# Destinations of sorted expert rows from one load and a one-hot product, one register for three tiles, nine result buffers, the shared expert last

## The chip, the cores and the metric

The kernel runs on 1 core of one Trainium2 chip. The metric is device microseconds of one execution. Three runs of the kernel before gave 907.51, 905.93 and 907.47 us, median 907.47. A profile covers one further execution; its times count from the start of its span. Engines: TensorE (PE, its weight loads PEld), VectorE (DVE), ScalarE (ACT), GpSimd (POOL) and SyncE (SP). SP computes nothing here: it issues most of the DMAs. "SPq" is its queue.

## The reference

One transformer block, B = 8 batches of 256 channels by 512 values; for the second half each channel is one token of width 512.

```python
x = x + cross_attention(layernorm(x), ctx, mask)            # 16 heads of 16, softmax over 512 source positions
flat = layernorm(x).reshape(-1, 512)                        # 2048 tokens
shared = sigmoid(flat @ shared_gate.T) * (flat @ shared_up.T) @ shared_down.T      # float32, hidden 352
weights = softmax(flat @ router_w.T)                        # 8 experts
top_w, top_idx = top_k(weights, 2)
routed = sum over e of comb[:, e] * (sigmoid(xb @ wg[e].T) * (xb @ wu[e].T)) @ wd[e].T   # bfloat16
return x + layernorm(x) + shared + routed                   # as the kernel's accumulator holds it: acc = x + norm(x)
...
```

Every token goes through the shared expert; of the eight routed experts it needs only its two.

## The kernel before

**Attention.** Steps are numbered by (G, h): G = 0 to 31 is a quarter of a batch's heads, h = 0 to 7 a step in it. A step does one `row_max` (L416: a score product of two matmuls into one PSUM bank, then DVE's maximum, L424) for a coming group, one `exp_scores` (L438) for this group, and on some steps `attend`, the projections or the parts of the feed-forward work of the batch before. `row_max` R = 8 (G+1) + h + LEAD runs LEAD = 2 steps ahead. A `plan` of 32 lists a batch hands out the further work: `spread` (L949) puts the items of `shared_units` (one item is one matmul group of the shared expert, 30 per batch) and of `route` (the routing of a batch) on chosen steps. For the last batch the steps of the shared expert's first 24 items stand in SOONER (L944); the other six follow behind the attention (L1112 to L1117).

**Sorting.** For the first 15 half batches of tokens (NS = 15, 128 tokens each) `route` works out, on DVE, each token's two experts and its two rows in a list sorted by expert. `place` (L643) then scatters with indirect DMAs from POOL: the token's 512 bfloat16 values to `xs`, and two words, its place in the result and its weight, to the same row of `whose`. The 16th half batch isn't sorted. `expert_map` (L666) works out for each of NT = 37 tiles of 128 sorted rows its expert (packed eight to a register) and its first row (`M["row"]`, L715).

**Tiles.** `expert_tiles` (L719) goes over the 37 tiles. `fetch(t)` (L727) runs on SP's queue: it loads first rows into registers in pieces (L733: 2, 8, 12 and 15 of them), then issues a transposing DMA of the tile (L739, `late_ctx<-xs`, four buffers, three tiles ahead), and a small DMA of the tile's 128 places and weights (L741, `whom<-whose`, six buffers). `gate_up_of` (L757) does the two products `eg` and `eu` and DVE's gated product `hz` (L771), `turn_h` (L778) turns `hz` on PE (L781), `down_of` (L788) multiplies by the down weights (`ey`, L795), ACT scales by the weight (L802) and POOL scatters the rows to `zs` (L803, traced as L201). PE's order is gate and up of t, down of t-2, turn of t-1.

**The end.** `give_back` (L818): POOL loads 12 accumulators back (`again`, L833, 256 KB each); `results(n)` (L835) loads the two result rows of 128 tokens from `zs` (three buffers, on SP, L837); `add` (L839) adds them on DVE (L842) and the write of the output follows on SP (L844). The order at the end is: 37 tiles; the shared expert of the last batch (L864, L915; 12 products of 4 matmuls, then two halves of 3); then the 16th half batch, dense, through all eight experts (`dense`, weights applied on ACT, L775, and DVE, L776), summed in one PSUM bank. The additions start in the middle of the shared expert and are placed by estimated time: at most 28 of the 30 during the shared expert, one for each 0.78 us of estimated PE work. `again` is issued at one per round of three items from round six on.

PSUM banks for the tiles come from a ring of six (`bank`, L80). One call of `bank` moves it on by one.

Of the kernel before, what the change touches and what calls it, by code (L numbers as in the profile page):

```python
# [36 lines left out]
def xattn_ffn_kernel(  # L37
# [137 lines left out]
    for i in range(8):  # L175
        nc.gpsimd.memset(eights[:, i : i + 1], float(8**i))
    tv = const.tile([P, NT], F32, name="tv")
    nc.gpsimd.iota(tv, [[1, NT]], channel_multiplier=0, allow_small_or_imprecise_dtypes=True)
# [11 lines left out]

    xs = dram.tile([E * ROWS + P, T], BF16, name="xs")
    whose = dram.tile([E * ROWS + P, 2], I32, name="whose")
    gu16 = dram.tile([E, 2, I, T], BF16, name="gu16")
# [356 lines left out]
    def route(b, tts=(0, 1)):  # L550
# [61 lines left out]
        def share():  # L612

            w16 = one.tile([P, n, E], BF16, tag=f"r{n}_comb16", name="comb16")
            nc.vector.tensor_copy(w16, t["w"])
            part = one.tile([P, 2, n, E], F32, tag=f"r{n}_part", name="part")
            nc.vector.scalar_tensor_tensor(part, both, 0.5, of_choice(w16), ALU.mult, ALU.mult)
            t["who"] = who = two.tile([P, 2, n, 2], I32, tag=f"r{n}_who", name="who")
            nc.vector.reduce_sum(who[:, :, :, 1].bitcast(F32), part, axis=AX.X)
            nc.vector.tensor_scalar(  # L620
                who[:, :, :, 0], place0[:, :, tts[0] : tts[0] + n], float(b * C), None, ALU.add
            )
            t["h16"] = h16 = one.tile([P, n, E], BF16, tag=f"r{n}_h16", name="h16")
            nc.vector.tensor_add(h16, t[0], t[1])
# [36 lines left out]

    PACKED = (NT + 7) // 8
    NEXT = [base0]
    M = {}

    def expert_map():  # L666
# [39 lines left out]
        def rows():  # L706
            step = sm("step", [E - 1])
            nc.vector.tensor_sub(step, t["shift"][:, 1:], t["shift"][:, : E - 1])
            past = t["past"]
            nc.vector.tensor_mul(past, past, row8(step).to_broadcast([P, NT, E - 1]))  # L710
            r = sm("r", [NT])
            nc.vector.reduce_sum(r, past, axis=AX.X)
            nc.vector.scalar_tensor_tensor(r, tv, float(P), r, ALU.mult, ALU.subtract)
            M["row"] = ri = one.tile([P, NT], I32, tag="m_ri", name="ri")
            nc.vector.tensor_scalar(ri, r, float(E * ROWS), None, ALU.min)  # L715

        return [(0.0, f) for f in (tiles, ends, experts, rows)]

    def expert_tiles():  # L719

        XT, HT, WHO = {}, {}, {}
        AHEAD = 3
        PIECES = [(0, 2), (2, 10), (10, 22), (22, NT)]
        ROW, EIGHT = {}, {}
        whole = {}

        def fetch(t):  # L727

            if t >= NT:
                return  # L730
            for first, end in PIECES:
                if t == first:
                    _, rs = nc.values_load_multi_w_load_instructions(  # L733
                        M["row"][0:1, first:end], engines=(mybir.EngineType.SP,), min_val=0, max_val=E * ROWS
                    )
                    ROW.update(zip(range(first, end), rs))
            row = ROW.pop(t)
            XT[t] = late("ctx")[:, t % 4, :].rearrange("p (k n) -> p k n", n=P)
            nc.sync.dma_start_transpose(out=XT[t], in_=xs[bass.ds(row, P), :])  # L739
            WHO[t] = six.tile([P, 2], I32, tag="who", name="whom")  # L740
            nc.sync.dma_start(out=WHO[t], in_=whose[bass.ds(row, P), :])  # L741

# [14 lines left out]
        def gate_up_of(t):  # L757
            whole.pop(t, None)
            xT = XT.pop(t) if t < NT else S[B - 1]["xTb"]
            pg = bank([P, I], F32, "eg")  # L760
            pu = bank([P, I], F32, "eu")
            for m, ps in ((0, pg), (1, pu)):
                for kc in range(NKC):
                    nc.tensor.matmul(  # L764
                        ps, xT[:, kc, :], weights_of(t, guT, m, kc, slice(None)),
                        start=(kc == 0), stop=(kc == NKC - 1),
                    )
            th = two.tile([P, I], F32, tag="th", name="eth")
            nc.scalar.activation(th, pg, AF.Tanh, scale=0.5)  # L769
            if t < NT:  # L770
                nc.vector.scalar_tensor_tensor(HZ[t % 2], th, 1.0, pu, ALU.add, ALU.mult)  # L771
                fetch(t + AHEAD)
            else:
                w = S[B - 1]["comb"][:, 0, t - NT : t - NT + 1]
                nc.scalar.activation(th, th, AF.Identity, scale=w, bias=w)  # L775
                nc.vector.tensor_mul(HZ[t % 2], th, pu)  # L776

        def turn_h(t):  # L778
            ps = bank([P, 3, P], BF16, "pht")
            for ic, (i0, n) in enumerate(ECH):  # L780
                nc.tensor.transpose(ps[:, ic, :], HZ[t % 2][:, i0 : i0 + n], identb)  # L781
            HT[t] = two.tile([P, 3, P], BF16, tag="hT", name="hT")
            if t < NT:
                evacuate(HT[t], ps)
            else:
                nc.scalar.copy(HT[t], ps)

        def down_of(t):  # L788
# [10 lines left out]
            if t < NT:  # L799
                y = (late("mb", 2)[:, t % 5, :] if t % 5 < 2 else late("xm")[:, t % 5 - 1, :])  # L800
                who = WHO.pop(t)
                nc.scalar.activation(y, ps, AF.Copy, scale=who[:, 1:2].bitcast(F32))  # L802
                scatter(zs, who[:, 0:1], y, bounds_check=2 * ROWS - 1, oob_is_err=False)  # L803

# [10 lines left out]

        return lambda: [fetch(t) for t in range(AHEAD)], stream(0, NT), stream(NT, NT + E)

    def give_back():  # L818
# [9 lines left out]
        byrow = zs.rearrange("(c r) t -> r c t", c=2)  # L828
        Z = {}

        def again(b, tt):
# [3 lines left out]
        def results(n):  # L835
            Z[n] = three.tile([P, 2, T], BF16, tag="extra", name="z")
            nc.sync.dma_start(out=Z[n], in_=byrow[n * P : (n + 1) * P])  # L837

        def add(n, c):  # L839
            b, tt = halves[n]  # L840
            a = S[b]["acc", tt]
            nc.vector.tensor_add(a, a, Z[n][:, c, :])  # L842
            if c == 1:
                nc.sync.dma_start(out=out[b, tt * P : (tt + 1) * P, :], in_=a)  # L844

# [6 lines left out]
    def shared_units(b, own):  # L852
# [58 lines left out]
        def down(tt, ic):  # L911
# [6 lines left out]
            if ic == 2:  # L918
                acc = s["acc", tt]
                nc.vector.scalar_tensor_tensor(acc, t["y"], 0.5, acc, ALU.mult, ALU.add)  # L920
                if b < NB - 1:
                    nc.sync.dma_start(out=ACC[b][tt], in_=acc)

        return (
# [20 lines left out]
        (8, 2), (9, 2), (10, 1), (11, 3),  # L945
        (13, 2), (15, 3), (17, 2), (19, 3), (21, 3), (23, 2), (25, 1),
    ]
# [63 lines left out]
    nc.gpsimd.memset(blank, 0.0)  # L1011
    nobody = five.tile([P, E * NS + 1, 2], I32, tag="acc", name="nobody")
    nc.gpsimd.memset(nobody, NOWHERE)

# [13 lines left out]
    for b in range(B):  # L1028
# [15 lines left out]
        elif b == B - 1:  # L1044
# [4 lines left out]
            sorted_last = route(b, (0,)) + expert_map()  # L1049
            fetch, tiles, dense = expert_tiles()  # L1050
            spread(plan, sorted_last, [(23, 1), (24, 1), (25, 2), (26, 3), (27, 2), (28, 2), (29, 2), (30, 1)])
            plan[30].append(fetch)
        later = plan[STEPS:]
        plan = plan[:STEPS]
        for g in range(NG):
            G = NG * b + g
            for h in range(8):
                st, half = divmod(h, 2)
                R = 8 * (G + 1) + h + LEAD
                if R // 8 < last:  # L1060
                    row_max(R // 8, (R % 8) // 2, R % 2)
                exp_scores(G, st, 1 - half, "s2" if R // 8 < last else ("s1", "s2")[h % 2])
# [52 lines left out]
    residual(B - 1, 1)  # L1115
    token_stats(B - 1, 1)
    some(units, 3)  # L1117
    some(tiles, 3)
    token_norm(B - 1, 1, nc.vector)
    some(tiles, 3)  # L1120
    turn_tokens(B - 1, 1)
    short = deque(route(B - 1, (1,)))
    again, results, adds = give_back()
    n = 0
    while tiles:
        some(tiles, 3)
        n += 1
        if n >= 2:
            some(short, 1)
        if n >= 6 and again:  # L1130
            again.popleft()()
    assert not short and not again
    for _ in range(3):
        results.popleft()()
    done, due = 0.0, 7.0
    todo = shared_units(B - 1, False)
    todo = [
        (sum(us for us, _ in todo[i : i + n]), lambda fs=todo[i : i + n]: [f() for _, f in fs])
        for i, n in [(4 * k, 4) for k in range(6)] + [(24, 3), (27, 3)]
    ]  # L1140
    for i, (us, go) in enumerate(todo + dense):
        if i == len(todo):
            ring.remove(0)
        go()
        done += us
        while adds and done > due and (i >= len(todo) or len(adds) > 2):
            due += 0.78
            adds.popleft()()
            if results and len(adds) % 2 == 0:
                results.popleft()()  # L1150
    while adds:
        adds.popleft()()
    acc = S[B - 1]["acc", 1]
    nc.vector.tensor_add(acc, acc, M["sum"])
    nc.sync.dma_start(out=out[B - 1, P:, :], in_=acc)

# [32 lines left out]
```

## Time and profile before

| quantity | value |
|---|---|
| median of 3 runs | 907.47 us |
| profiled execution: time, span | 907.82 us, 906.0 us |
| mean granted PE clock | 0.987 |
| busy PE, DVE, ACT, POOL | 839.3, 579.6, 370.1, 310.1 us |
| first `eg` of the tiles | 754.63 us |
| end of the last `ey` of the 37 tiles | 862.56 us |
| shared expert of the last batch | 862.40 to 878.96 us |
| dense half batch, to its last product | 879.03 to 902.02 us |
| last addition, issue of its write, end | 902.06, 902.78, 906.0 us |

Busy time of PE is the length of its matmuls and not its use at full speed. The stages of most interest are the last 150 us, where the granted clock and the releasers of waits are read per stage.

### The profile page before, as it was taken

The numbers are of one execution on the slowest core, as the hardware profiler recorded it, in microseconds if no ns is written. First come the engines' busy times: TensorE is split into PE (matmuls) and PEld (weight loads), VectorE is DVE, ScalarE is ACT, GpSimd is POOL, SyncE is SP. The second block draws the span as 40 slices with busy tenths as digits, with TensorE's granted clock in tenths as the row PEclk, the third lists the DMA queues.
The fourth block names the chain that finished last, engine by engine and source line by source line (L and its number), as shares of the span: only waits on it lengthen the run. The fifth ranks groups of instructions, "written<-read, shape, count | busy, mean of one in ns | idle before, by whom it ended". The sixth has DMA issues, their size and how long they took to land.

```text
span 906.0 us, 13498 instructions
## 1 busy us (share of the span) xinstructions
PE 839.3 (93%) x4931; PEld 336.2 (37%) x4943; DVE 579.6 (64%) x1068; ACT 370.1 (41%) x482; POOL 310.1 (34%) x375
## 2 busy tenths in 40 slices
PE   6888989999999999999999999999999999887986
PEld 3322323343334333433343334333433324444463
DVE  6676766766776767676767686768676644322246
ACT  3244434343434343434443434343434442444524
POOL 2114305270537053705270616062601311453400
PEclk9899999999999999999999999999999989999999
DMA  5149713122812281228122600110000002584346
GB/s 172 45 135 352 260 17 91 17 56 44 179 22 56 48 179 19 56 47 180 19 56 44 137 1 24 33 49 1 24 12 13 24 24 59 105 178 98 84 138 222
DMA packets 99097, 75.24 MB, mean 83 GB/s; under 512 B 65645, under 2 KB 86543, under 8 KB 98648
## 3 DMA queue, kind: packets, MB, share of 16 engines
q1 hardware_dynamic: 92168, 53.63, 22.7%
q0 software_dynamic: 5904, 19.70, 10.2%
q10 hardware_dynamic: 960, 1.05, 0.3%
q8 instruction: 40, 0.66, 0.3%
q14 instruction: 25, 0.20, 0.1%
HBM read 38.02 MB, written 40.79 MB: 87 GB/s over the span
## 4 chain that ended last, share of the span: by engine, by line
PE 68%; DVE 18%; issue 6%; DMA 3%; POOL 3%; SPq 1%; ACT 1%; ACTq 0%; DVEq 0%; POOLq 0%
PE s L422 23%; DVE nm L424 9%; PE av L460 9%; PE psy L915 5%; PE pu L864 4%; PE psq L399 4%; PE eu L764 3%; PE psk L399 3%; PE eg L764 3%; PE ey L795 3%; PE pgu L864 2%; PE psv L367 2%; PE s L445 2%; DVE q L406 2%; PE pg L864 2%
## 5 line engine op out<-in xcount | busy, mean ns | idle before, releaser
L447 ACT ACTIVATE e<-s 128x1024 f32<-128x1024 f32 x256 | 261.9, 1023 | 406.0 <-PE s L445 405.8
L424 DVE TENSOR_REDUCE nm<-s 128x2 f32<-128x1024 f32 x256 | 313.2, 1223 | 145.3 <-PE s L445 133.0
L422 PE MATMUL s<-k,q 32*128 32x512 f32 x1024 | 290.2, 643 | 27.9 <-DVE nm L424 25.0
L445 PE MATMUL s<-q,k 32*128 32x512 f32 x1024 | 289.9, 647 | 0.0
L460 PE MATMUL av<-e,V 128*32 128x512 f32 x1024 | 139.5, 609 | 0.2 <-ACT e L447 0.2
L422 PEld LDWEIGHTS s<-k,q 32*128 32x128 f32 x1024 | 77.0, 183 | 134.2 <-DVE nm L424 114.0
L390 POOL TENSOR_SCALAR extra<-mb,alpha,beta 128x512 f32<-128x512 f32 x60 | 45.6, 764 | 176.4 <-DVE q L406 176.1
L332 POOL TENSOR_TENSOR rs<-ve,mhalf 128x1 f32<-128x1 f32 x32 | 18.2, 568 | 210.3 <-DVE ve L330 208.0
L445 PEld LDWEIGHTS s<-q,k 32*128 32x128 f32 x1024 | 76.8, 184 | 5.1 <-issue 4.3
L771 DVE SCALAR_TENSOR_TENSOR hz<-eth,eu 128x352 bf16<-128x352 f32 x37 | 19.2, 520 | 65.4 <-PE eu L764 59.4
L460 PEld LDWEIGHTS av<-e,V 128*32 128x32 f32 x1024 | 20.5, 108 | 100.7 <-issue 97.1
L915 PE MATMUL psy<-sdT,h 128*128 128x512 f32 (+1 forms) x96 | 48.0, 615 | 0.8 <-DVE h L876 0.8
L201 POOL DMA_INDIRECT xs<-xnb,at x30 | 29.9, 996 | 51.3 <-DVE at L649 27.2
L764 PE MATMUL eg<-guT,late_ctx 128*128 x148 | 31.7, 319 | 12.4 <-DMA late_ctx<-xs 9.7
L764 PEld LDWEIGHTS <-late_ctx 128*128 128x128 bf16 x296 | 28.2, 99 | 35.7 <-DMA late_ctx<-xs 9.7
L864 PE MATMUL pu<-xT,sguT 128*128 128x256 f32 x128 | 36.2, 401 | 0.7 <-ACT th L872 0.7
L769 ACT ACTIVATE eth<-eg 128x352 f32<-128x352 f32 x45 | 21.0, 467 | 38.1 <-PE eg L764 36.6
L367 PE MATMUL psv<-WvT,ctx 128*128 128x256 f32 x128 | 35.7, 402 | 0.0
L764 PE MATMUL eu<-guT,late_ctx 128*128 x148 | 35.3, 320 | 0.0
L864 PE MATMUL pg<-xT,sguT 128*128 128x256 f32 x128 | 35.0, 400 | 0.0
L864 PE MATMUL pgu<-xT,sguT 128*96 128x256 f32 (+1 forms) x128 | 34.1, 392 | 0.0
L399 PE MATMUL psq<-xm,WqT 128*128 128x512 f32 x64 | 33.0, 641 | 0.0
(186 smaller groups left out, 969.5 us busy)
## 6 DMA issues: line engine op xcount, KB each, us to landing
xs<-blank SPq DMA_DIRECT2D x7, 1920.0 KB, 13.6
ctx<-in_ctx_dram SPq DMA_DIRECT2D x8, 512.0 KB
z<-zs SPq DMA_DIRECT2D x15, 256.0 KB, 3.1
x<-in_x_dram SPq DMA_DIRECT2D x7, 512.0 KB, 3.8
accd<-acc SPq DMA_DIRECT2D x12, 256.0 KB, 2.5
again<-accd POOLq DMA_DIRECT2D x12, 256.0 KB, 3.6
out_dram<-again SPq DMA_DIRECT2D x12, 256.0 KB, 2.7
gu<-in_L_ffn_w_gate_dram POOLq DMA_DIRECT2D x8, 352.0 KB, 4.4
```

What stands on the lines that cost most here:

```text
L201: i = nc.gpsimd.indirect_dma_start(to[:, :], bass.IndirectOffsetOnAxis(ap=rows, axis=0), what, None, **bounds).ins
L367: nc.tensor.matmul(ps, ct[:, kc, sc * P : (sc + 1) * P], WvT[:, kc, :], start=(kc == 0), stop=(kc == 1))
L390: engine.tensor_scalar(t, S[b]["mb"], at, be, ALU.mult, ALU.add)
L399: nc.tensor.matmul(ps, W[:, kc, g // 2].rearrange("p j a d -> p (j a d)"), rhs[:, kc, :], start=(kc == 0), stop=(kc == 1),)
L422: nc.tensor.matmul(ps[:, jj, :], q[r, tci * P : (tci + 1) * P], k[r, :], start=True, stop=True)
L424: best = lambda: nc.vector.reduce_max(NM[G % 2][:, tci, c0 : c0 + 33 : 32], ps, axis=AX.X)
L445: nc.tensor.matmul(ps[:, jj, :], k[r, sc * P : (sc + 1) * P], q[r, :], start=True, stop=True)
L447: nc.scalar.activation(e, ps, AF.Exp)
L460: nc.tensor.matmul(AVT[G][32 * j : 32 * j + 32, :], V[:, sc, 2 * g + j // 2, j % 2 : j % 2 + 2, :].rearrange("p o d -> p (o d)"), et[j // ...
L764: nc.tensor.matmul(ps, xT[:, kc, :], weights_of(t, guT, m, kc, slice(None)), start=(kc == 0), stop=(kc == NKC - 1),)
L864: lambda kc=kc: nc.tensor.matmul(ps, sguT[:, m, kc, i0 : i0 + n + more], s["xT"][:, kc, :], start=(kc == 0), stop=(kc == NKC - 1))
L915: nc.tensor.matmul(t["y"], t["h"][:n, ic, tt * P : (tt + 1) * P], sdT[:n, ic, :], start=(ic == 0), stop=(ic == 2))
```

## The change

The destinations and weights of all sorted rows are loaded once (`whose`, 121 groups of 128 rows, to `rows`), and a product with a one-hot matrix picks those of each tile (`whom`); the small DMA of each tile goes. First rows, divided by 128, are packed three to a register in base 128, and one register is loaded for three tiles. The dense half batch follows the 37 tiles in the same stream; its weights are applied by turning `hz` with a diagonal matrix. The shared expert of the last batch comes after it. Results have nine buffers, six of them never used twice; they are requested together. Output writes of the first 14 half batches go through POOL; the last batch's follow its shared expert. `again` is issued in every third round. SOONER puts five items later, and in group 0 `row_max` runs one step later up to step 5, which does two.

```diff
+    thirds = const.tile([P, 3], F32, name="thirds")
+    for i in range(3):
+        nc.gpsimd.memset(thirds[:, i : i + 1], float(P ** (i - 1)))
+    ncol = const.tile([P, 1], F32, name="ncol")
+    nc.gpsimd.iota(ncol, [[0, 1]], channel_multiplier=P, allow_small_or_imprecise_dtypes=True)
...
-            M["row"] = ri = one.tile([P, NT], I32, tag="m_ri", name="ri")
-            nc.vector.tensor_scalar(ri, r, float(E * ROWS), None, ALU.min)
+            nc.vector.tensor_scalar(r, r, float(E * ROWS), None, ALU.min)
+            packed = sm("r3", [THIRDS, 3])
+            nc.vector.tensor_mul(packed, r3, row8(thirds).to_broadcast([P, THIRDS, 3]))
+            p = sm("p3", [THIRDS])
+            nc.vector.reduce_sum(p, packed, axis=AX.X)
+            M["row"] = ri = one.tile([P, THIRDS], I32, tag="m_ri", name="ri")
+            nc.vector.tensor_copy(ri, p)
...
+            if t % 3 == 0:
+                _, (v,) = nc.values_load_multi_w_load_instructions(
+                    M["row"][0:1, t // 3 : t // 3 + 1], engines=(mybir.EngineType.SP,), min_val=0, max_val=P**3 - 1
+                )
+                ROW[t // 3] = v
+            v = ROW[t // 3]
+            row = (v // P ** (t % 3)) % P * P if t % 3 else v % P * P
             XT[t] = late("ctx")[:, t % 4, :].rearrange("p (k n) -> p k n", n=P)
             nc.sync.dma_start_transpose(out=XT[t], in_=xs[bass.ds(row, P), :])
-            WHO[t] = six.tile([P, 2], I32, tag="who", name="whom")
-            nc.sync.dma_start(out=WHO[t], in_=whose[bass.ds(row, P), :])
+        def whom():
+            n = E * NS + 1
+            rows = one.tile([P, P, 2], F32, tag="m_rows", name="rows")
+            nc.sync.dma_start(out=rows[:n], in_=whose.rearrange("(n p) w -> n p w", p=P))
+            pick = one.tile([P, NT], F32, tag="m_pick", name="pick")
+            nc.vector.tensor_scalar(pick[:n], M["r"][:n], ncol[:n], None, ALU.is_equal)
+            def go():
+                ps = bank([P, 2, NT], F32, "pwho")
+                for w in range(2):
+                    nc.tensor.matmul(ps[:, w], rows[:n, :, w], pick[:n], start=True, stop=True)
+                M["to"] = to = one.tile([P, NT], I32, tag="m_to", name="to")
+                nc.vector.tensor_copy(to, ps[:, 0])
+                M["weight"] = weight = one.tile([P, NT], F32, tag="m_weight", name="weight")
+                nc.vector.tensor_copy(weight, ps[:, 1])
+            M["whom"] = go
...
+                if t < NT:
+                    nc.tensor.transpose(ps[:, ic, :], h, identb)
+                else:
+                    nc.tensor.matmul(ps[:, ic, :], h, M["diag"][:, t - NT, :], start=True, stop=True)
...
+        def weighted():
+            M["diag"] = diag = one.tile([P, E, P], BF16, tag="u", name="diag")
+            for e in range(E):
+                nc.vector.tensor_scalar(diag[:, e, :], identb, S[B - 1]["comb"][:, 0, e : e + 1], None, ALU.mult)
...
+        for i in range(2):
+            z = two.tile([P, 3, 2, T], BF16, tag="V", name="z3")
+            Z.update((3 * i + j, z[:, j]) for j in range(3))
...
-            if c == 1:
-                nc.sync.dma_start(out=out[b, tt * P : (tt + 1) * P, :], in_=a)
+            if c == 1 and b < B - 1:
+                nc.gpsimd.dma_start(out=out[b, tt * P : (tt + 1) * P, :], in_=a)
...
+                if b == B - 1:
+                    nc.sync.dma_start(out=out[b, tt * P : (tt + 1) * P, :], in_=acc)
...
-        (13, 2), (15, 3), (17, 2), (19, 3), (21, 3), (23, 2), (25, 1),
+        (13, 1), (15, 2), (17, 2), (19, 2), (21, 1), (23, 2), (25, 2), (26, 1), (27, 1), (28, 1), (29, 1),
...
+                lead = LEAD if G or h > 5 else LEAD - 1
+                for R in range(8 * (G + 1) + h + lead, 8 * (G + 1) + h + lead + (2 if G == 0 and h == 5 else 1)):
+                    if (G or h) and R // 8 < last:
+                        row_max(R // 8, (R % 8) // 2, R % 2)
...
     token_stats(B - 1, 1)
+    M["whom"]()
     some(units, 3)
...
-    n = 0
-    while tiles:
+    n = 2
+    while n <= NT:
         some(tiles, 3)
         n += 1
-        if n >= 2:
+        if n >= 4:
             some(short, 1)
-        if n >= 6 and again:
+        if n % 3 == 0 and again:
             again.popleft()()
...
-    for _ in range(3):
-        results.popleft()()
-    done, due = 0.0, 7.0
+    todo = list(tiles) + [(0.0, added)] + [
...
+    done, due = 0.0, 6.5
+    for i, (us, go) in enumerate(todo):
         go()
         done += us
+        if i == 0:
+            for _ in range(9):
+                results.popleft()()
+        while adds and done > due:
+            due += 0.82
             adds.popleft()()
             if results and len(adds) % 2 == 0:
                 results.popleft()()
+        if i == len(todo) - 3:
+            while adds:
+                adds.popleft()()
```

`added` adds the dense sum to the second accumulator of the last batch; the list `todo` ends with the eight groups of the shared expert's items. `weighted` follows the last item of `route` for the 16th half batch.

## The prediction

> **What bounds the kernel now.** I read the busy table by stages first. Up to 750 us PE is busy 95% and more in nearly every stretch at full clock: the attention is bound by PE, and the change gives it no work back. The last 150 us are different. I asked for the chain that ended last from 800 us on (start, length, what):
>
> ```profile
> 801.11 6.12 DMA late_ctx<-xs
> ...
> 810.95 3.25 SPq L733
> ...
> 818.19 3.25 DMA late_ctx<-xs
> 821.43 0.21 issue
> 821.65 1.33 PE eg L764 x4
> ```
>
> The end hangs on the tile's load: once a transposing DMA took 6.12 us, once SP loaded fifteen registers, and the load behind them was issued only at 818.19. SP's queue in order of time shows the same for the piece of twelve:
>
> ```profile
> 773.44 0.34 SPq L741 DMA_DIRECT2D whom<-whose  x1
> 779.71 1.22 SPq L739 DMA_TRANSPOSE late_ctx<-xs  x1
> ```
>
> From the end of one row to the start of the next are 5.93 us. For fifteen it is 7.28, for eight 3.93 (746.68 to 750.61): (7.28-3.93)/7 = 0.48 us a register and next to nothing fixed. Then the busy table in stretches of 4 us (PE, PEld, DVE, ACT, POOL, granted clock, DMA share, GB/s):
>
> ```profile
> 784.00:788.00 4.00, 3.85 (x15) 1.83 (x14) 0.76 (x3) 1.39 (x3) 0.00 (x0) 0.63 0.92 104
> ...
> 800.00:804.00 4.00, 3.19 (x18) 1.54 (x18) 0.52 (x1) 1.60 (x4) 2.26 (x3) 1.00 1.20 194
> ...
> 820.00:824.00 4.00, 2.35 (x9) 1.28 (x10) 0.00 (x0) 0.46 (x1) 0.00 (x0) 0.64 0.44 98
> ```
>
> After each register stall the granted clock is 0.63 to 0.64 for a while, and around 800 us the DMA engines are full: that is where the twelve `again` loads are issued, one each 2.4 us. Last, the waits of SP's queue (us in total, times, longest), and the DMAs (us to landing at the end):
>
> ```profile
> SPq L844 <- DVE again L842: 17.4, 11, 3.4
> ...
> SPq L741 <- DMA zs<-late_mb,whom: 9.9, 9, 3.3
> ```
> ```profile
> z<-zs SPq DMA_DIRECT2D x15, 256.0 KB, 3.1
> again<-accd POOLq DMA_DIRECT2D x12, 256.0 KB, 3.6
> out_dram<-again SPq DMA_DIRECT2D x12, 256.0 KB, 2.7
> ```
>
> Each output write makes SP wait for DVE, with the next result load queued behind it; and `whom` waits for an older scatter, because its buffer comes free with that.
>
> **The change, part by part.** All terms are against the profiled execution: span 906.0, time 907.82, so 1.8 us around the span; its time is 0.35 above the median.
>
> *Tile loads.* I listed the starts of the turns (L781), one per tile. Undisturbed they are 2.39 us apart (829.93 to 856.22, eleven tiles). The excess over that: 5.57 us around 783 (two tiles took 10.35), 0.56, 1.19 and 1.80 from 799 to 810, 5.37 at 824.89; together 14.5 us, of which the waits list gives 9.7 as PE waiting for `late_ctx`, the rest is refilling and slow clock. In the new order SP does per tile one transpose (1.2 us), a third of a 0.48 us register, and two or three register steps for the packed row. No such step is in SP's trace; the check steps behind L733 take about 0.25 us a register, so 0 to 0.75; I take 0.5, the middle of a small range. That is 1.9 us against 2.39, so SP stays ahead. A load is issued when its buffer comes free, three tiles or 7.2 us before use, and needs 2.7. `again` at one per 7.2 us moves 36 GB/s where it now moves 109. I take 2 us as left over: gain 12.5, at least 6 (only the two register stalls' PE waits, 3.3+4.2 less 1.5), at most 14.5.
>
> *One load and the product.* Added: on DVE a memset, the multiply, the reduction and the comparison (rows of such size: 0.09 to 0.20), 0.7 us ahead of the first fetch. That is covered: the first `eg` starts at 754.63, while its tile was issued at 742.87. The load of 121 KB can go out after the third fetch, about 747.2. Nearest rows: 1 KB in 2.0 us, 256 KB in 3.1, so it lands by about 750.3. PE wants it about 751.0, before the last six shared matmuls. Behind the product in PE's queue stands everything, so each us late is a us lost: 0 to 1.5, and I take 0. The Trainium skill, "DMA: Bandwidth & Descriptors", section "Why a DMA increments its semaphore by 16 and not by 1", says that a load issued from SP runs on the largest number of engines up to 16 that divides its partition count. That speaks against 121 partitions (11 engines): by it my estimate is 2.0 + 1.1x(121/256)x(16/11) = 2.8 us, landing at 750.4, still in time; no DMA of 121 partitions is in this trace. The four small float32 matmuls cost 0.3 us (the eight `psr` ones take 0.8 to 1.0). Against it, the extra call of `bank` moves the ring: the first `eg` no longer gets the bank that DVE's L920 still reads, a wait of 0.78. Net gain 0.5, between -1.5 and 0.8.
>
> *The end.* Now: from 862.56 to 906.0, 43.4 us. New, PE's own work after the 37 tiles: eight dense tiles at 2.13 (882.42 to 884.55, where nothing disturbed them; ACT's second pass of 0.68 is gone, the turn by a diagonal matrix has the size of the old one) = 17.0; the shared expert 16.55; the last addition 0.7; write and end 3.25 (902.78 to 906.0): 37.5. DVE beside it: `todo` begins after the last scatter's product; from the last `ey` to the first landed result it now takes 6.06 us (862.56 to 868.62), and the first addition is due after 6.5. Additions of 0.69 each 0.82 leave DVE 0.13 for each; with `hz` (0.52) a dense tile needs 2.37 us of DVE against 2.13 of PE for four tiles, a lag of 1 us that the order of the turns hides. The last seven additions are flushed between the shared product `h` and its down matmuls: 0.69+4.83+0.69+0.69 = 6.9 on DVE against PE's 0.74+5.42+0.69 = 6.9. Level, but results 12 to 14 have only three buffers and are asked for late: result 14 some 1.5 us into the flush, landed 3.1 to 4.5 later, 0.5 to 1.9 us over. I take 1.2: the end is 38.7, gain 4.7. Ends: 2 us more if the second drain of the tile pipeline (1.15+0.62 idle now at 860) shortens; 3 us loss if results and writes, 320 GB/s at this pace against 313 in the best 3 us now, fall behind. The rule that stands against moving the writes to POOL is in the same page, section "Issuing engines are not separate DMA queues": issuing from several engines saves only the sequencer's issue time. By it this part would be worth 14 x 0.35 us of SP, none of it on the path; the row of 17.4 us says that SP waits in front of loads. My sum does not need to choose, since it takes PE's work as the bound.
>
> *`weighted`*: eight DVE passes over 128x128 (0.25 each by L495) in one go, 2 us ahead of one `hz` whose slack is about 1.2: cost 0.4, 0 to 2.
>
> *Group 0.* Now `row_max` R 10 at 31.62 holds the bank; the next waits 1.31 us for DVE, PE's clock is 0.57 from 32 to 40, and two groups of matmuls take 2.08 instead of 1.13. New: one `row_max` there, so no such wait, and PE goes on to the V product. But step 5 does two in a row with 1.3 us between. Waits even out, the slow clock (0.95+0.95+0.5) goes: gain 2.5, from -1.5 to 4.
>
> *SOONER.* Five matmul groups move to steps 25 to 29, where PE waits 1.42 us for the routing chain (L632 for L624) and runs at clock 0.58 to 0.74 from 735 to 745, some 2.9 us. They fill the wait: gain 1.5 (a third), from -2 to 4.5.
>
> *Constants*: four instructions on POOL at 3.4 us, under 0.4 us, ahead of a wait of 0.33 us for DVE: nothing, at most 0.4.
>
> Sum: -12.5 -0.5 -4.7 +0.4 -2.5 -1.5 = -21.3; span 884.7, time 886.5.
>
> **Rivals.**
> *Tail by DMA and DVE* (17%): results and writes don't hold the pace; additions stand in front of `hz` and of the shared products in DVE's order, and PE idles and loses its clock. For: 0.93 to 0.95 DMA share in the best stretches now; against: nine requests outstanding instead of three. Price: the end 3 to 7 us later, 889.5 to 893.5.
> *Loads still late* (12%): the transposes are slow of themselves, or SP's register steps and the order behind them cost more than 0.75 us. For: 2.7 us median even at low DMA share; against: no stall from 826 to 858 with `again` over. Half or more of the 12.5 stays: 893 to 899.
> *Slower* (5%): POOL's queue carries the fourteen writes one at a time. At 3.6 us each they need 50.4 from about 857, and the last two behind them end beyond 911, a time of 913. It decides when one write takes over 3.3 us of the queue. Against: `again` was issued each 2.4 us while each took 3.6, so they overlap.
> *It does nothing* (3%): gains in the middle are eaten by waits in front of `pwho` and at step 5, and the end is bound as now; about 906 to 909.
>
> **How the numbers follow.** My forecast, 882 to 889, has 58%; better than 882, with the top of the group 0 and SOONER ranges, 5%. A range of 879 to 897 leaves out the slower and the idle case, the worst of late loads and the very best, about 15%. Differences under 0.2% can't be told from none here. Faster 0.93, same 0.02, slower 0.05.
>
> **What would show it.** Turns of the 37 tiles 2.4 us apart throughout, no gap over 2 us on SP; `eg` waiting for `late_ctx` under 2 us in all; granted clock 1.00 from 760 on; eight dense tiles 2.1 to 2.2 apart directly behind; results landing in under 4.5 us; the last DVE addition no more than 2 us behind PE's last product; PE at full clock at 35 us, and no 1.4 us wait at L632. I am wrong if `pwho` waits, if DVE waits for `z` while PE waits for `hz`, or if the stalls of the tile loads only move.

## The result and the profile after

| | before | after | forecast |
|---|---|---|---|
| median of 20 runs, us | 908.3 (905.17 to 918.76) | 899.02 (894.1 to 908.38) | 886.5 (879 to 897) |
| profiled execution: time, span, us | 907.82, 906.0 | 898.62, 896.8 | 886.5, 884.7 |
| mean granted PE clock | 0.987 | 0.986 | |

The ratio is 0.9897 (95%: 0.9875 to 0.9919). The kernel became faster by 1%, where 2.3% was forecast: of some 21 us, 9.2 are seen in the two profiled executions. Line numbers from here on are those of the changed kernel, or of the experiment named.

I laid the two traces side by side at points that both have: the product that turns the row maxima of each group (`psn`, L438; that of a later group stands in step 6 of the group before it), the first down product `psy` of the shared expert behind the attention, the first `eg`, the end of the last `ey`, the end of the span. The differences of these distances add up to the difference of the spans:

| stretch | before | after | after - before | forecast |
|---|---|---|---|---|
| start to the first `psn` | | | -0.7 | 0 |
| group 0 (first `psn` to group 1's) | 26.58 | 32.57 | **+6.0** | -2.5 |
| groups 1 to 29 | | | -1.4 | 0 |
| group 30, and group 31 to the late `psy` (SOONER) | | | -2.9 | -1.5 |
| late `psy` to first `eg` (load and product) | 7.73 | 13.87 | **+6.1** | -0.5 |
| 37 tiles | 107.93 | 94.17 | -13.8 | -12.5 |
| end of the last `ey` to the end | 43.44 | 40.91 | -2.5 | -4.7 |
| sum | 906.0 | 896.8 | -9.2 | -21.3 |

The forecast's sum also holds `weighted`, +0.4, which has no row. I count the first and third rows as scatter: a first load landed a little sooner, and in groups 10 and 14 two waits of 0.7 us did not occur again. The one edit that falls into the third row, an item of SOONER in group 29, shows nothing there (20.92 us in both).

**The tile loads** went as forecast. The tiles before stood in stalls with the clock at 0.63 to 0.64; the same stretches in the table of 4 us of the changed kernel (columns as in the prediction):

```profile
784.00:788.00 4.00, 4.00 (x23) 1.89 (x21) 1.40 (x7) 2.34 (x5) 1.85 (x2) 1.00 0.52 101
800.00:804.00 4.00, 3.65 (x23) 1.90 (x22) 1.18 (x3) 1.75 (x4) 1.84 (x3) 1.00 0.45 107
820.00:824.00 4.00, 3.66 (x24) 1.90 (x22) 0.88 (x2) 2.30 (x5) 1.17 (x2) 1.00 0.68 132
```

Full clock in each, 23 or 24 matmuls in place of 9 to 18, and at 800 us a DMA share of 0.45 in place of 1.20. The turns of the tiles are 2.1 to 2.9 us apart, but for two of 3.9 and 3.7 among the first five. No wait of PE for `late_ctx` is left. What PE waited for from 740 us on (us in total, times, longest):

```profile
PE pwho L764 <- DMA rows<-whose: 3.6, 1, 3.6
PE psy L956 <- DVE h L917: 2.3, 1, 2.3
PE eg L793 <- issue: 1.4, 4, 0.4
```

The first two rows are the two losses at the end. The order of time shows how the first one arises (start, length; the bracket gives the idle time before it and its releaser):

```profile
742.61 0.69 DVE L917 SCALAR_TENSOR_TENSOR h<-th,pu 128x512 f32<-128x512 f32 x1 [2.67 <-PE pu L905]
...
747.59 0.17 DVE L728 CAST ri<-p 128x13 int32<-128x13 f32 x1
...
748.95 4.05 SPq L751 DMA_TRANSPOSE late_ctx<-xs  x3
...
753.10 0.52 SPq L757 DMA_DIRECT2D rows<-whose  x1
...
755.61 1.04 PE L764 MATMUL pwho<-pick,rows 121*128 121x37 f32 x4 [3.60 <-DMA rows<-whose]
756.46 5.47 PE L956 MATMUL psy<-sdT,h 128*128 128x512 f32 x6
...
761.72 0.84 PE L793 MATMUL eg<-guT,late_ctx 128*128 x4
```

The load leaves at 753.10, behind the register and three transposes, and not at 747.2 as I had it. PE stands at `pwho` for 3.6 us, and then works slowly: the six `psy` take 5.47 us, where they take 2.83 undisturbed (the run with the load first, below). The clock of the stretch behind the wait:

```profile
756.00:760.00 4.00, 4.00 (x8) 1.95 (x8) 0.30 (x2) 0.00 (x0) 0.00 (x0) 0.50 0.14 33
```

**Group 0** lost its time to the clock more than to waits. The stretches from 34 to 42 us, first of the kernel before, then of the changed one:

```profile
34.00:38.00 4.00, 3.93 (x8) 1.68 (x8) 1.24 (x2) 0.00 (x0) 0.00 (x0) 0.50 0.00 0
38.00:42.00 4.00, 4.00 (x17) 1.47 (x20) 1.93 (x4) 1.02 (x1) 0.00 (x0) 0.82 0.00 0
```
```profile
34.00:38.00 4.00, 4.00 (x10) 1.18 (x8) 1.83 (x3) 0.00 (x0) 0.00 (x0) 0.50 0.00 0
38.00:42.00 4.00, 4.00 (x8) 1.35 (x8) 0.00 (x0) 1.02 (x1) 0.00 (x0) 0.54 0.00 0
```

From 14 to 50 us PE waits 3.3 us for DVE's maxima in the kernel before and not in the changed one, as forecast; but the half clock stays, and stays longer. Then step 5 does its two row maxima, PE waits for the first of them, and the clock falls a second time:

```profile
55.00 0.97 PE L427 MATMUL s<-k,q 32*128 32x512 f32 x2 [1.33 <-DVE nm L429]
```
```profile
54.00:58.00 4.00, 3.00 (x11) 1.36 (x12) 2.08 (x2) 1.02 (x1) 0.00 (x0) 0.66 0.00 0
```

**The end.** Dense tiles run 2.01 us apart (forecast 2.13). Then results 12 to 14 come late:

```profile
880.56 5.54 SPq L878 DMA_DIRECT2D z<-zs  x3
882.50 0.69 DVE L883 TENSOR_TENSOR again<-again,z 128x512 f32<-128x512 f32 x1 [1.96 <-DMA z<-zs]
883.11 0.68 DVE L917 SCALAR_TENSOR_TENSOR h<-th,pu 128x512 f32<-128x512 f32 x1
883.84 7.12 PE L956 MATMUL psy<-sdT,h 128*128 128x512 f32 x12 [2.31 <-DVE h L917]
```

DVE waits 1.96 us for a result, with the shared expert's `h` queued behind that addition; PE waits 2.31 us for `h`, and its twelve `psy` then take 7.12 us (clock 0.59 from 884 to 888 us) where the kernel before took 5.42.

### The profile page after: what moved, and what is told of

Its sections match the earlier page's. It is cut to its first block, busy times and chain, and to the rows that moved or that the text cites. A ratio compares the mean times of both kernels' runs of the same rounds, so it can differ in the third digit from the quotient of the medians.

```text
span 896.8 us, 13356 instructions
## 1 busy us (share of the span) xinstructions
PE 844.5 (94%) x4947; PEld 340.3 (38%) x4947; DVE 580.9 (65%) x1083; ACT 364.3 (41%) x474; POOL 317.9 (35%) x393
## 3 DMA queue, kind: packets, MB, share of 16 engines
q1 hardware_dynamic: 84956, 50.04, 21.3%
## 4 chain that ended last, share of the span: by engine, by line
PE 72%; DVE 16%; issue 5%; POOL 3%; DMA 2%; SPq 1%; ACT 0%; DVEq 0%; ACTq 0%; POOLq 0%
PE s L427 23%; DVE nm L429 9%; PE av L465 9%; PE psy L956 4%; PE eu L793 4%; PE psq L404 4%; PE pu L905 3%; PE eg L793 3%; PE ey L823 3%; PE psk L404 3%; PE psv L372 3%; PE s L450 3%; PE pgu L905 3%; PE pg L905 2%; DVE q L411 2%
## 5 line engine op out<-in xcount | busy, mean ns | idle before, releaser
L427 PE MATMUL s<-k,q 32*128 32x512 f32 x1024 | 290.9, 644 | 24.3 <-DVE nm L429 21.3
L465 PE MATMUL av<-e,V 128*32 128x512 f32 x1024 | 137.5, 605 | 0.2 <-ACT e L452 0.2
L799 DVE SCALAR_TENSOR_TENSOR hz<-eth,eu 128x352 bf16<-128x352 f32 x45 | 23.4, 521 | 56.7 <-PE eu L793 49.3
L465 PEld LDWEIGHTS av<-e,V 128*32 128x32 f32 x1024 | 20.4, 108 | 98.1 <-issue 94.7
L956 PE MATMUL psy<-sdT,h 128*128 128x512 f32 (+1 forms) x96 | 52.3, 665 | 2.3 <-DVE h L917 2.3
L411 DVE SCALAR_TENSOR_TENSOR q<-psq,mine,extra 128x512 f32<-128x512 f32 x32 | 22.6, 746 | 15.6 <-PE psq L404 15.6
L206 POOL DMA_INDIRECT whose<-who,at x30 | 28.8, 961 | 9.1 <-issue 8.8
```

The costliest lines, as they stand in the source:

```text
L206: i = nc.gpsimd.indirect_dma_start(to[:, :], bass.IndirectOffsetOnAxis(ap=rows, axis=0), what, None, **bounds).ins
L427: nc.tensor.matmul(ps[:, jj, :], q[r, tci * P : (tci + 1) * P], k[r, :], start=True, stop=True)
L465: nc.tensor.matmul(AVT[G][32 * j : 32 * j + 32, :], V[:, sc, 2 * g + j // 2, j % 2 : j % 2 + 2, :].rearrange("p o d -> p (o d)"), et[j // ...
L956: nc.tensor.matmul(t["y"], t["h"][:n, ic, tt * P : (tt + 1) * P], sdT[:n, ic, :], start=(ic == 0), stop=(ic == 2))
```

## Theory and rival before the experiments

My theory: the steps of the change are worth what was forecast, and three separate losses of 12 to 15 us in all cover them: the new order in group 0, the late load in front of `pwho`, and results 9 to 14 held up by their buffers. Each can be undone alone. Rivals: group 0 lost its time to chance and not to its order; the product is late because of the load itself (121 rows, few engines) and not because of its place; the end is held up by the writes on POOL's queue and not by the buffers. A further question was which of the edits to the tile loads made the 13.8 us.

Chips differ: the median of the kernel before was 926.35 us on the chip of the first four runs, 906.82 on that of `e4_sooner`, `e5_again`, `e7_regs` and `e6_all`, 907.84 on that of the other four. So times are compared with the kernel before on the same chip, as ratios to it, and stretches within a profile. The intervals of the ratios are 0.4 to 1.2% wide, about as much as a single loss is worth; the stretches carry the readings.

## The experiments

Each edit is made in the changed kernel, unless said otherwise.

**The changed kernel again** (`a0_after`), no edit.

> The changed kernel once more, unaltered, for a second profile. Theory (each loss has its place in the code): in the first group the distance from the first to the second product of the row maxima (L438) is again 32.6 us as in the profile of after (28.27 to 60.84), where before had 26.6; PE again waits about 3.6 us for the rows of the destinations (L764). Rival (chance: PE's clock happened to be granted late in that one execution): the distance falls back to 27 to 28 us. Time 895 to 901 us in both.

Ratio 0.9971 (0.9934 to 1.0008): on this chip, which is slower for both kernels, these runs show no gain that is clear of noise. Stretches as above: group 0 32.51, late `psy` to first `eg` 13.43, tiles 93.98, end 40.41. The losses are no accident of one execution.

**Group 0 as before** (`e1_lead`).

```diff
-                lead = LEAD if G or h > 5 else LEAD - 1
-                for R in range(8 * (G + 1) + h + lead, 8 * (G + 1) + h + lead + (2 if G == 0 and h == 5 else 1)):
-                    if (G or h) and R // 8 < last:
-                        row_max(R // 8, (R % 8) // 2, R % 2)
+                R = 8 * (G + 1) + h + LEAD
+                if R // 8 < last:
+                    row_max(R // 8, (R % 8) // 2, R % 2)
```

> The changed kernel with the first group's order of row maxima as before. Theory: the distance between the first two L438-type products is 26.6 us again, and the time is 6.0 us below that of the changed kernel. Rival (chance of the clock): the distance and the time are as in the changed kernel, within 1 us.

Group 0 takes 26.81 us; ratio 0.9875 (0.9821 to 0.993). The clock is no better:

```profile
30.00:34.00 4.00, 1.14 (x8) 0.34 (x8) 2.69 (x3) 0.96 (x1) 0.00 (x0) 0.91 0.02 4
34.00:38.00 4.00, 3.74 (x8) 1.68 (x8) 1.43 (x2) 0.06 (x1) 0.00 (x0) 0.50 0.00 0
```

So the old order waits (PE busy 1.14 of 4 us) and then runs at half clock, too, yet it is 5.7 us shorter than `a0_after`.

**The load of the rows first** (`e2_rows_first`).

```diff
-            plan[30] += [fetch, whom]
+            plan[30] += [whom, fetch]
```

> The changed kernel with the load of all destinations ahead of the first three tile loads in SP's queue. Theory (the load is late because it stands behind the register and three transposes of 1.35 us each): it is issued by 748.5 on the scale of the after profile instead of 753.1, PE doesn't wait for it, the six shared matmuls behind take 2.9 us instead of 5.5, and the time is 6 us lower. Rival (the load must wait for the last scatter of destinations, or for the late map on DVE, wherever it stands): PE still waits 2 us or more, gain under 2 us.

Late `psy` to first `eg` 7.04 us, 0.7 below the kernel before; ratio 0.9864 (0.9824 to 0.9903). SP and PE in order of time:

```profile
773.82 0.32 SPq L757 DMA_DIRECT2D rows<-whose  x1
...
780.35 0.56 PE L764 MATMUL pwho<-pick,rows 121*128 121x37 f32 x4
780.74 2.83 PE L956 MATMUL psy<-sdT,h 128*128 128x512 f32 x6
783.40 0.76 PE L793 MATMUL eg<-guT,late_ctx 128*128 x4
```

The load left 6.5 us before the product that uses it, and that has no wait. Its size was not at fault: in the changed kernel it took 2.5 us from issue to the product (753.10 to 755.61).

**Six more result buffers** (`e3_zbuf`), in a pool that is free by then:

```diff
+            if n in (9, 12):
+                z = two.tile([P, 3, 2, T], BF16, tag="V", name="z3")
+                Z.update((n + j, z[:, j]) for j in range(3))
```

> The changed kernel with results 9 to 14 in the six buffers that come free first (those of results 0 to 5) instead of three buffers of results 6 to 8. Theory (the end waits for results that are asked for late, because their buffers are the last to come free): result 9 is requested about 7 us earlier, DVE waits under 1 us for results in place of 4.0, PE doesn't wait 2.3 us for the shared product, and the time is 3 to 4.6 us lower. Rival (the DMA engines are the bound there, full at 350 GB/s): waits move to other results, time within 1 us.

The end takes 37.37 us in place of 40.4 to 40.9, with the writes still on POOL's queue, and 0.1 us off the 37.5 that PE's own work and the last write had come to. Ratio 0.9921 (0.9885 to 0.9957). This run showed by chance what the clock is worth in group 0. It has the new order, but its clock held:

```profile
34.00:38.00 4.00, 3.74 (x14) 1.36 (x12) 2.16 (x4) 1.02 (x1) 0.00 (x0) 1.00 0.00 0
38.00:42.00 4.00, 4.00 (x21) 1.52 (x20) 2.54 (x3) 1.02 (x1) 0.77 (x1) 1.00 0.16 40
```

and its group 0 took 26.64 us. At full clock, then, the new order needs no longer than the old one does at half clock; no profile has the old order at full clock. Against this run, the changed kernel loses 4.6 us up to the first `av` product (L465), in the first slow stretch, and 1.3 us behind the wait of step 5. My reading, which no run takes apart: in the old order DVE's maxima set the pace and PE has idle time to lose, while the new one keeps PE busy and is slowed by what the clock takes. The old order hides only so much: in `e8_all_sp_writes` the clock was at half from 18 to about 52 us, and its group 0 took 29.06 us; the new order with the clock at half from 18 to 51 us (`e5_again`) took 32.06.

**SOONER as before** (`e4_sooner`).

```diff
-        (13, 1), (15, 2), (17, 2), (19, 2), (21, 1), (23, 2), (25, 2), (26, 1), (27, 1), (28, 1), (29, 1),
+        (13, 2), (15, 3), (17, 2), (19, 3), (21, 3), (23, 2), (25, 1),
```

> The changed kernel with the shared expert's items on the attention's steps as before (SOONER). Two effects are to be told apart. Theory: the late map on DVE (728 to 759 lines, 6 us later in after than in before, because the shared product's DVE pass now stands in front of it) makes the load of destinations late, so with the old steps the load is issued before PE wants it, the wait of 3.6 us at L764 and the slow clock behind it go (6 us), while 0 to 3 us come back as waits for the routing chain (L637): net 3 to 6 us lower. Rival (the place in SP's queue behind three transposes alone makes it late): the wait at L764 stays above 2 us and the time rises by 0 to 3 us.

Late `psy` to first `eg` 7.15 us, without touching the load's place; ratio 0.9878 (0.9846 to 0.9911). The wait for the routing chain is back:

```profile
PE psc L637 <- DVE h L629: 1.4, 1, 1.4
```

This joins two terms that I had costed apart. The items moved by SOONER bring the shared expert's DVE pass (L917 at 742.61, after a wait of 2.67 us for PE) into the middle of the sorted map on DVE, where before it came at 731.47, ahead of the routing; the last row of the map starts at 747.59 in place of 741.11, and behind it everything on SP. Some 1 us of this is no effect of SOONER: the first late `psy` also starts 0.95 us later.

**`again` as densely as before, from the ninth round** (`e5_again`).

```diff
-        if n % 3 == 0 and again:
+        if n >= 8 and again:
```

> The changed kernel with the accumulators' loads one per round from round eight on (12 rounds in a row, as dense as before) instead of every third. Theory A (the stalls of the tiles before came from register loads, and from full DMA engines around 800 us): the 37 tiles, first gate product to last down product, take 94.2 us now and would take 97 to 99, with PE waiting 2 to 4 us for late_ctx in the rounds with the loads. Theory B (only the registers and the wait of the small load for older scatters mattered): 94 to 95 us.

Tiles 94.16 us, no wait for `late_ctx`; ratio 0.9927 (0.9899 to 0.9956). In the changed kernel the twelve loads in a row, which I had made a part of the stalls, cost nothing; beside register stops and small loads they weren't tried.

**First rows in pieces of 2, 8, 12 and 15 again** (`e7_regs`).

```diff
-            if t % 3 == 0:
-                _, (v,) = nc.values_load_multi_w_load_instructions(
...
+            for first, end in [(0, 2), (2, 10), (10, 22), (22, NT)]:
+                if t == first:
+                    _, rs = nc.values_load_multi_w_load_instructions(
```

> The changed kernel with the first rows in pieces of 2, 8, 12 and 15 registers as before, all else as changed. Theory: SP's queue again stops for about 0.48 us a register, 5.9 and 7.3 us; without the small loads' waits SP starts these stops up to a tile earlier, so the 37 tiles take 98 to 105 us in place of 94.2. Rival (the small load's wait for scatters was what made the register loads harmful; with three tiles of lead the stop alone is hidden): 94 to 96 us.

Tiles 97.73 us, 3.6 more; the wait at `pwho` grows to 7.2, since the registers stand in front of the load on SP. Two runs, 904.96 and 919.07 us, too few for a ratio; the stretches are what this one tells.

**The small load of each tile again, without the product** (`e9_small_dma`); the packed registers stay.

```diff
+            WHO[t] = six.tile([P, 2], I32, tag="who", name="whom")
+            nc.sync.dma_start(out=WHO[t], in_=whose[bass.ds(row, P), :])
...
-            plan[30] += [fetch, whom]
+            plan[30] += [fetch]
```

> The changed kernel with the small load of places and weights per tile back in place of the one load and the product; registers stay packed. With e7 (registers alone back: 37 tiles in 97.7 us, 3.6 more than the changed kernel, of 13.8 more before) this splits the gain of the tiles. Theory (the two made each other worse: the small load's wait for an older scatter ate the lead that would have hidden the register stops): alone it costs 1 to 4 us, 95 to 98 us, so that the two singles sum to clearly less than 13.8. Rival (the terms add): 104 us.

Late `psy` to first `eg` 7.72 (as before the change, 7.73), tiles 98.98, 4.8 more than with the product. PE waits for `late_ctx`, and the cause stands on SP's queue (waits of PE, then of SP):

```profile
PE eg L795 <- DMA late_ctx<-xs: 3.1, 3, 1.8
```
```profile
SPq L753 <- DMA zs<-late_mb,whom: 3.5, 4, 1.4
SPq L753 <- DMA zs<-late_xm,whom: 3.4, 3, 1.8
```

Registers alone cost 3.6 us and the small load alone 4.8, but the kernel before, which has both and the dense `again`, 13.8: 5.4 us come only where they meet. The likely reason, read from SP's waits and not tested, is that the small load's waits for scatters use up the three tiles of lead that would carry SP over a register stop. Ratio 0.9872 (0.9813 to 0.993), two runs.

**All three losses undone** (`e6_all`): the edits of `e1_lead`, `e2_rows_first` and `e3_zbuf` together.

> The changed kernel with the first group's old order, the load of destinations first in SP's queue, and results 9 to 14 in the buffers that come free first. Theory (three separate losses that add up): 6.0 at most at the first group (only where PE's clock is slow there), 6.4 at the product, 3.3 at the end; 12 to 15 us below the changed kernel on the same chip, 2.2 to 2.7% below the kernel before. Rival (they share one cause, the clock, and PE loses it elsewhere instead): less than 8 us below the changed kernel.

**884.54 us** (six runs, 882.5 to 886.21), ratio 0.9745 (0.9724 to 0.9767); span 881.6, mean clock 0.995. Group 0 26.86, late `psy` to `eg` 7.05, tiles 94.17, end 37.47. By the ratios it lies 1.5% below the changed kernel (0.9897), some 14 us, with the theory at 12 to 15. Its span is 24.4 us below that of the kernel before: tiles -13.8, end -6.0, SOONER -3.0, load and product -0.7, group 0 +0.3, and -1.3 of the rows that I count as scatter.

**The same, with the writes on SP** (`e8_all_sp_writes`).

```diff
-                nc.gpsimd.dma_start(out=out[b, tt * P : (tt + 1) * P, :], in_=a)
+                nc.sync.dma_start(out=out[b, tt * P : (tt + 1) * P, :], in_=a)
```

> The kernel of e6 with the writes of the first 14 half batches on SP's queue again, among the result loads. From the last down product of the 37 tiles to the end it takes 37.5 us in e6. Theory (with buffers that come free early, the loads behind a write wait only for an addition that is due anyway): 37.5 to 39, time within 1.5 us of e6. Rival (a write in front of a load costs the load its head start, as the 17.4 us of waits before suggested): 40 us or more.

The end takes 36.91 us against 37.47: with results asked for early, writes on SP cost nothing, although SP still waits 9.3 us for DVE in front of them. The row of 17.4 us, which the prediction set against the Trainium skill's rule ("DMA: Bandwidth & Descriptors", section "Issuing engines are not separate DMA queues"), is no cost here, and this run agrees with the rule. With three result buffers, as in the kernel before, it wasn't tried. Ratio 0.976 (0.9698 to 0.9823).

**The same, with the new group 0** (`e10_all_lead`), **and with SOONER as before** (`e11_all_sooner`).

> The kernel of e6 with the changed order of the first group's row maxima. Theory (at full clock the two orders take the same 26.6 us from the first to the second product of the maxima, but the new one gives PE nothing to wait for and so shows a slow clock in full, 32 us): the distance is 31 to 33 us in most executions, the time 3 to 6 us above e6, with a wider spread of the mean granted clock (e6: 0.991 to 0.995). Rival (the order doesn't matter, the slow clock came by chance): within 1.5 us of e6.

> The kernel of e6 with the shared expert's items on the steps of before. Theory: only the wait for the routing chain comes back (1.4 us at L637) less what the later steps cost; from the last product of the maxima to the end of the attention 23.0 us in place of 22.6, time 0 to 1.5 us above e6. Rival (the wait of 1.4 us lets PE's clock fall in most executions, as in the profile of before): 2 to 4 us above e6.

With the new group 0: group 0 32.51 us, 890.35 us, ratio 0.9783 (0.9743 to 0.9823). That is 0.4% above `e6_all` by the ratios, and 5.7 us above `e11_all_sooner`, which ran on the same chip with the old group 0 and the old SOONER. Its clock, as in the changed kernel:

```profile
34.00:38.00 4.00, 4.00 (x10) 1.17 (x8) 1.83 (x3) 0.00 (x0) 0.00 (x0) 0.50 0.00 0
38.00:42.00 4.00, 4.00 (x6) 1.17 (x4) 0.00 (x0) 1.02 (x1) 0.00 (x0) 0.50 0.00 0
```

With the old SOONER: the profile shows the 2.9 us of groups 30 and 31 back, the time does not (884.65 us, ratio 0.9726, 0.9687 to 0.9766, against 0.9745). So the gain from SOONER is seen in the trace only.

## Why the prediction was wrong, step by step

- **Tile loads, -12.5: right** (-13.8). The cause was half right. The register stops and the small load's waits make it, 5.4 us of it only where they meet; the full DMA engines around 800 us, which I read as a third cause, make nothing by themselves (`e5_again`).
- **One load and the product, -0.5: the step that failed first.** "The load of 121 KB can go out after the third fetch, about 747.2" took the map's end from the trace of before. SOONER, costed under its own heading, puts a DVE pass with a wait of 2.67 us into that map. The load left 5.9 us later, or 5 us counted from the first late `psy`, and the stretch lost 6.1 us, where my range ended at 1.5. That `pwho` waits was the first sign of being wrong that I had named. The product itself was costed rightly: with the load in time the stretch is 7.04 against 7.73, a gain of 0.7 (`e2_rows_first`). The estimate by the Trainium skill ("DMA: Bandwidth & Descriptors", section "Why a DMA increments its semaphore by 16 and not by 1"), 2.8 us for 121 partitions, stands beside a measured 2.5 from issue to product, which my interpolation gives without the factor for eleven engines; neither mattered.
- **"Each us late is a us lost": too cheap.** 3.6 us of waiting cost 6.8 (13.87 against 7.04), with the matmuls behind it at a clock of 0.50. The same at the end: 2.3 us of waiting for `h`, then 7.12 in place of 5.42.
- **The end, -4.7: mis-sized** (-2.5). I allowed 1.2 us for results 12 to 14; they cost 3.0 to 3.5 (40.41 and 40.91 against 37.37 in `e3_zbuf`), about half of it by the slow clock. PE's own bound of 37.5 was right to 0.1 by luck: in `e3_zbuf` the dense tiles take 15.1 us and not 17.0, and from the last `psy` to the end it is 5.5 us and not 3.95. Results landed after 4.5 us, at the far end of my 3.1 to 4.5.
- **Group 0, -2.5: wrong in sign** (+6.0). "Waits even out, the slow clock goes": the two waits of 2.0 and 1.3 us went, the clock did not, and the wait of 1.3 us at step 5, which I had named, came with a second slow stretch. I took a slow clock to go with the wait that stands next to it; the old order had been hiding it.
- **SOONER, -1.5:** the trace shows -2.9, besides the harm done to the load.
- **`weighted`, +0.4, and the constants:** nothing of them is seen.
- The rivals: "tail by DMA and DVE" took place in small (2.3 us of PE wait, not through the pace of writes); "loads still late" did not occur, although its 893 to 899 comes close to the time by chance; POOL's writes did not pile up. "It does nothing" (3%) named the places of two of the three losses, `pwho` and step 5, but neither SOONER behind the one nor the clock behind the other; and the gain of the tiles, which it had eaten up, was larger than both together.

Not settled: whether group 0 can be run without its half clock. Eight of nine profiles with the new order had it, and those with the old order too; what draws the one exception is not known.

## What to carry to other kernels

When one edit moves work on an engine, work out again the start times of every other edit that waits for that engine, before adding the terms: here a better place for five matmul groups made a load 5 us late, and swapping two entries of a list gave all of it back. Price a wait of PE above its length, for the clock that can fall behind it: here 3.6 us of waiting cost 6.8, 2.3 cost 4.0, and in group 0 the slow stretch cost more than its waits. Do not count on that clock returning because one wait is gone. And before work is put on an order that keeps PE busy, ask whether the idle time of the old order was covering a slow stretch.

## What the hardware showed unasked

- **The clock falls after short idle times, and not always.** In group 0 of the new order PE waits 0.78 us at its start and 1.33 us at step 5. Of nine profiled executions eight had the clock at 0.50 to 0.54 from 34 to 42 us (one of them, `e5_again`, from 18 us on), while `e3_zbuf` with the same code there had 1.00; behind the second wait it fell in six of the nine. The Trainium skill, "TensorE: Matmul & The Clock Gate", section "Part 1: The HAM clock gate (the "warmup" mystery)", says that the window in which activity is watched is free-running; such a draw agrees with it, though no run here shows the window itself.
- **Most scatter between runs goes with the clock.** Over the changed kernel's runs, a mean clock of 0.993 goes with 894.1 and 894.3 us, 0.986 with 898.6 to 899.9, 0.973 with 908.2 and 908.4: some 0.7 us for each 0.001.
- **Chips differ by 2%:** the kernel before takes 926.35 us on one and 906.82 on another; the changed kernel takes 925.59 on the first and 899.02 on a chip where the kernel before takes 908.3, so it loses more on the slower one. Its trace there (`a0_after`) has 24.4 us in place of 22.2 in groups 7, 11, 15 and 19, and 2.2 to 3.8 us more in groups 23, 27 and 30. What the kernel before loses where isn't known, since it has no trace from that chip.
